# A selective-scan kernel: buffers named by the written schedule, y stored by pieces, late loads planned with a longer landing

## The chip, the cores and the metric

The kernel runs on one core of a Trainium2 chip. The time is the device time of one execution in microseconds; the number quoted for a kernel is the median of its runs. A core has five engines that each work through their own queue of instructions in order: PE (TensorE: matmuls and transposes, with its weight loads shown apart as PEld), DVE (VectorE), ACT (ScalarE), POOL (GpSimd) and SP (SyncE, which here only issues DMAs). Sixteen DMA engines move the data between memory and SBUF.

## The reference

The input x is 8 images of 64 x 64 positions with 96 channels. The first layer is a state-space block on a group-normalised x:

```
xz = x @ in_proj_w.T;  xin, z = split(xz)                 # 192 channels each
xc = silu(depthwise_conv3x3(xin))
xs = [xc by rows, xc by columns, and both reversed]       # K = 4 directions, 4096 positions
dts, Bs, Cs = split(x_proj_weight[k] @ xs[k])             # 6 + 16 + 16 rows
delta = softplus(dt_projs_weight[k] @ dts + bias)
h[t] = h[t-1] * exp(delta[t] * A) + (delta[t] * u[t]) * B[t]    # for each of 192 channels and N = 16 states
y[t] = sum over n of h[t, n] * C[t, n]  + D * u[t]
out = (layernorm(sum of the four y) * silu(z)) @ out_proj_w.T
x = x + out
```

A second layer follows: linear attention without softmax, and a two-layer feed-forward net whose products are rounded to an 8-bit float. By far the most work is the recurrence of h: 8 images x 4 directions x 192 channels x 16 states, each over 4096 positions.

## The kernel before

**Three passes.** Pass 1 (`pass1`, L274) normalises, projects and convolves, and writes u (the input of the scan), z and xd (the rows of dts, B and C) to memory; B and dt are also written split into three bf16 parts ("split", L244). Pass 2 (`pass2`, L548) does the scans and writes y for each image in two orders, o = 0 (by rows) and o = 1 (by columns). Pass 3 (`pass3`, L939) reads y and z and does all the rest.

**Tiling of pass 2.** A tile has 128 channels on the partitions and T = 1024 positions. Two images (a pair) have 2 x 192 = 384 channels, which makes three chunks: c = 0 and c = 1 hold 128 channels of one image each, and c = 2 holds the last 64 of both. So there are 4 pairs x 3 chunks = 12 chunks. A chunk has 4 directions k (order o = k % 2; k = 2, 3 reversed) of 4 pieces each, in all 192 pieces of 16 states n. "Piece 189" counts from 0.

**One piece.** `prepare` (L596) loads xb (B in three bf16 parts) and u, lets PE bring B to the other axis (ACT copies it to bT), lets POOL form du = delta * u, and PE and ACT transpose it to duT. `deltas_of` (L645) loads xdt, and makes delta by a matmul and a softplus on ACT. Then for each state n:

- `decay` (L720): ACT forms da = exp(delta * a), 128 x 1024.
- `products` (L759): PE fills a PSUM buffer "wide" with delta*u*B. There are three ways. ACT (`scaled`, L730) or POOL (`scaled_by_pool`, L746) forms x or xg from duT and bT, and PE transposes it, 8 transposes, after which the scan reads it; or PE spreads B over the channels with two matmuls and DVE multiplies by du in place.
- `scan` (L783): DVE runs the recurrence with one scan instruction per state into h, and so empties the "wide" buffer.
- for each two states: `carries` (L807, ACT copies the last column for the next piece), `times_c` (L822, POOL multiplies h by C in the tile c, which `load_c` (L708) loaded with C's rows repeated over all partitions, 1 MB), and `sum_over_n` (L836, PE adds the products up in the PSUM tile acc by transposing matmuls).

`take_acc` (L878): when a piece's sum is whole, ACT copies acc to its place in the SBUF tile y0 or y1 (`ys[o]`). Directions 0 and 1 leave it there. Directions 2 and 3 begin their sum with what is there and write back the total; after the fourth piece, `store_y` (L894) stores the whole of `ys[o]`, all 4096 positions. That is 2 MB to one image in c < 2, in runs of 512 B, and 1 MB to each of two images in c = 2, in runs of 256 B. All DMAs of this pass go through SP's queue (the very first loads through POOL's).

**Late work.** The x projection of image 7 and the splits of images 5 to 7 are done inside pass 2, beside the scans, by `late_x_projection` (L678) and `late_split` (L700). They share two single buffers, "late" (ux, bs) and "late2" (xd, bq).

**The order of work.** Nothing is scheduled at run time. `weave` (L148) plays the kernel through as a plan: each unit is a generator that yields the engine it wants next, the cost in us, the delay until its result is to be had (0.3 where none is given) and, where it takes a buffer, the pool's `Slots`. At each step the unit that can begin first goes next, and its instructions are recorded. `InOrder` (L85) then ties each engine to exactly this order. `Slots.when` (L138) tells the plan when the next buffer is free; it takes buffers in rotation, so the buffer of the allocation `count` earlier:

```python
        return 0.0 if self.taken < self.count else self.ends.get(self.taken + 1 - self.count)
```

The plan doesn't name the buffer, though: `take` (L571) asks the framework's pool of `bufs=count` for a tile, and the pool chooses by its own account. There are 4 da, 3 h, 4 x, 1 xg, 6 c, and in PSUM 3 wide and 1 acc (L556). Where the plan sees PE idle, `keep_busy` (L583) adds matmuls with a zero weight.

Of the kernel before, what the change touches and what calls it, by code (L numbers as in the profile page):

```python
# [39 lines left out]
PSUM = bass.MemoryType.PSUM  # L40
DRAM = bass.MemoryType.DRAM

P = 128
NB, HH, WW, C = 8, 64, 64, 96
# [7 lines left out]
NPC = L // T  # L52
NT = T // P
# [16 lines left out]
def chunk_rows(pair, c):  # L70

    b0 = 2 * pair
    if c < 2:
        return [(slice(0, P), b0 + c, slice(0, P))]
    return [(slice(64 * j, 64 * j + 64), b0 + j, slice(P, DI)) for j in range(2)]
# [9 lines left out]
class InOrder:  # L85


    def __init__(self, tc, engine):
        self.tc, self.engine, self.last = tc, engine, None
# [42 lines left out]
class Slots:  # L132
# [5 lines left out]
    def when(self):  # L138

        if self.held:  # L140
            return None
        return 0.0 if self.taken < self.count else self.ends.get(self.taken + 1 - self.count)

    def release(self, which, end):
        self.ends[which] = end


def weave(units, room, finished, between=None):  # L148

    free, clock = {}, 0.0
    waiting = {kind: [u for u in units if u[0] == kind] for kind in room}
    opened, ended, active = {kind: 0 for kind in room}, {kind: set() for kind in room}, []
    while True:  # L160
        for kind, todo in waiting.items():
            while opened[kind] < len(todo) and (opened[kind] < room[kind] or opened[kind] - room[kind] in ended[kind]):
                _, rank, unit = todo[opened[kind]]
                active.append([clock, rank, kind, opened[kind], unit, next(unit)])
                opened[kind] += 1
        best = None
        for at in active:
            while at[5][0] not in ENGINES and at[5] in finished:
                at[0] = max(at[0], finished[at[5]])
                at[5] = at[4].send(None)  # L170
            if at[5][0] not in ENGINES or (len(at[5]) > 3 and at[5][3].when() is None):
                continue
            begin = at[0] if len(at[5]) < 4 else max(at[0], at[5][3].when())
            key = (max(begin, free.get(at[5][0], 0.0)), at[1])
            if best is None or key < best[0]:
                best = key, at
        if best is None:
            assert not active and all(opened[kind] == len(todo) for kind, todo in waiting.items())
            return
        at = best[1]  # L180
        engine, cost, delay = (*at[5], 0.3)[:3]
        if len(at[5]) > 3:
            at[5][3].taken += 1
        clock = best[0][0]
        if between is not None:
            between(engine, clock - free.get(engine, 0.0))
        free[engine] = clock + cost
        at[0] = clock + cost + delay
        try:
            at[5] = at[4].send(at[0])  # L190
        except StopIteration:
            active.remove(at)
            ended[at[2]].add(at[3])
# [47 lines left out]
    return (a_neg, dsum, dt_b, dt_w, sel, sel2), load_dt_w  # L241


def split(engines, pool_of, cost, src, row, rows, pieces, at, dst):  # L244

    act, pool, sp = engines
    wide, used = GRP, rows * pieces
    yield "sp", 0.7, 4.0
    bq = pool_of.tile([P, wide], F32, name="bq", tag="late2")
    src = src[row : row + rows].rearrange("r (s t) -> (r s) t", s=pieces)  # L250
    sp.dma_start(bq[0:used], src[:, at : at + wide])
    yield "act", 0.6
    bs = pool_of.tile([P, NS, wide], BF16, name="bs", tag="late")
    act.copy(bs[0:used, 0, :], bq[0:used])
    yield "pool", cost
    pool.tensor_sub(bq[0:used], bq[0:used], bs[0:used, 0, :])
    yield "act", 0.6
    act.copy(bs[0:used, 1, :], bq[0:used])
    yield "pool", cost
    pool.tensor_sub(bs[0:used, 2, :], bq[0:used], bs[0:used, 1, :])  # L260
    yield "sp", 0.9
    half = used // 2
    for k2 in range(2):
        to = dst[k2].rearrange("e n (s t) -> (n s) e t", s=pieces)[:, :, at : at + wide]
        sp.dma_start(to, bs[half * k2 : half * (k2 + 1)])


def splits(b, o, b_d, dt_d):

    return [(0, 2 * N, 4, at, b_d[b][o]) for at in (0, GRP)] + [(DT0, 2 * R, 8, 0, dt_d[b][o])]  # L270
# [3 lines left out]
def pass1(ctx, tc, g, load_dt_w, ident, mhalf, engines, w_xp, u_d, z_d, xd_d, b_d, dt_d):  # L274
    nc = tc.nc
    pe, dve, act, pool = engines
    sp = InOrder(tc, nc.sync)
# [3 lines left out]
    two = ctx.enter_context(tc.tile_pool(name="p1two", bufs=2))  # L281
# [242 lines left out]
    def after(key, unit):  # L524
        yield key
        yield from unit

    units = []
    for pair in range(NB // 2):
        batches = (2 * pair, 2 * pair + 1)  # L530
        for b in batches:
            units += [("stats", statistics(b, q)) for q in range(NG)]
            units.append(("norm", group_norm(b)))
            units += [("proj", projection(b, q)) for q in range(NG)]
        for c in ORDER:
            units.append(("conv", convolution(pair, c)))
        for b in batches:
            for o in range(2 if b < LATE_X else 0):
                units += [("xproj", x_projection(b, o, q)) for q in range(NG)]
                if b < LATE:  # L540
                    units += [("split", after(("xd", b, o), split((act, pool, sp), two, 4.4, xd_d[b][o], *w))) for w in splits(b, o, b_d, dt_d)]
    units.append(("later", later_loads()))
    room = {"later": 1, "proj": 4, "norm": 1, "stats": 3, "xproj": 4, "split": 2, "conv": 3}
    weave([(kind, (list(room).index(kind), i), unit) for i, (kind, unit) in enumerate(units)], room, done)
# [3 lines left out]
def pass2(ctx, tc, g, ident, engines, fixed, w_xp, u_d, xd_d, b_d, dt_d, y_d):  # L548
# [3 lines left out]
    pe, dve, act, pool = engines  # L552
    sp = InOrder(tc, nc.sync)
    two = ctx.enter_context(tc.tile_pool(name="p2two", bufs=2))
    three = ctx.enter_context(tc.tile_pool(name="p2three", bufs=SOFT + 1))
    room = {"da": 4, "h": 3, "x": 4, "xg": 1, "c": 6, "wide": 3, "acc": 1}  # L556
    slots = {name: Slots(count) for name, count in room.items()}
    pools = {
        name: ctx.enter_context(tc.tile_pool(name=f"p2{name}", bufs=count, **({"space": PSUM} if name in ("wide", "acc") else {})))
        for name, count in room.items()  # L560
    }
    pieces = [
        (pair, c, k, NPC - 1 - i if k >= 2 else i) for pair in range(NB // 2) for c in range(3) for k in range(K) for i in range(NPC)
# [6 lines left out]

    def take(name, shape, dtype=F32):  # L571

        return pools[name].tile(shape, dtype, name=name), slots[name].taken

    def one_more(key, of, end):
        counts[key] = counts.get(key, 0) + 1
# [101 lines left out]
    def late_x_projection(b, o, q):  # L678

        yield "scans", 0  # L680
        pair, j = b // 2, b % 2
        cols = slice(q * GRP, (q + 1) * GRP)
        yield "sp", 1.8, 4.0
        ux = one.tile([P, 2, GRP], F32, name="ux", tag="late")
        sp.dma_start(ux[:, 0, :], u_d[b][o][0:P, cols])
        for i in range(2):
            sp.dma_start(ux[64 * i : 64 * i + 64, 1, :], u_d[2 * pair + i][o][P:DI, cols])
        yield "pe", 1.5, 0.2, slots["wide"]
        px, slot = take("wide", [P, T])
        for i, ty in enumerate((0, 1 + j)):  # L690
            pe.matmul(px[:, 0:GRP], w_xp[:, ty, o, :], ux[:, i, :], start=i == 0, stop=i == 1)
        end = yield "act", 0.58, 0.2
        xd = one.tile([P, GRP], F32, name="xd", tag="late2")[0 : 2 * NXD]
        act.copy(xd, px[0 : 2 * NXD, 0:GRP])
        slots["wide"].release(slot, end)
        end = yield "sp", 0.7, 3.0
        sp.dma_start(xd_d[b][o][:, cols], xd)
        one_more(("xd", b, o), NG, end)

    def late_split(b, o, which):  # L700

        yield "scans", 0
        if b >= LATE_X:
            yield "xd", b, o
        yield from split((act, pool, sp), one, 1.25, xd_d[b][o], *which)
        one_more(("split", b), 6, 0.0)

    def load_c(at, m):  # L708
# [169 lines left out]
    def take_acc(at):  # L878
        pair, c, k, pc = pieces[at]
        o = k % 2  # L880
        yield "sum", at
        end = yield "act", 0.95, 0.1
        if at % (K * NPC) == 0:
            for i in range(2):
                ys[i] = one.tile([P, NBLK, P], F32, name=f"y{i}")
        acc, slot = made["acc"]
        dst = ys[o][:, pc * NT : (pc + 1) * NT, :]
        act.copy(dst, acc)
        slots["acc"].release(slot, end)
        if k >= 2 and at % NPC == NPC - 1:  # L890
            yield "sp", 7.5, 6.0
            store_y(ys[o], o, chunk_rows(pair, c))

    def store_y(y, o, parts):  # L894
        for part, b, ch in parts:
            if o == 0:
                sp.dma_start(y_d[b][0].rearrange("(i p) d -> p i d", p=P)[:, :, ch], y[:, :, part])
            else:

                rows = y_d[b][1].rearrange("(h i w) d -> w h i d", w=2, h=HH)  # L900
                for w in range(2):
                    sp.dma_start(rows[w][:, :, ch], y[w * HH : (w + 1) * HH, :, part])

    units = []
    for at, (pair, c, k, pc) in enumerate(pieces):
# [334 lines left out]
```

## Time and profile before

| | us |
|---|---|
| median of 3 runs | 9894.99 (9894.46 to 9900.35) |
| profiled execution | 9906.51 |
| its span | 9904.5 |
| pass 1, until DVE's first scan | 683.5 |
| scans of pass 2 (683.5 to 9209.1) | 8525.6 |
| from the last scan to the end | 695.4 |

In the span DVE is busy for 94%, ACT for 92%, POOL for 91%, PE for 80%. The scans take 2.32 us each with a carried start value (2304 of them) and 2.26 us without (768); POOL's product with C takes 4.55 us (1536). The granted PE clock is 0.963 in the mean.

A line of a wait list reads: engine and what it writes, "<-" what ended the wait, total us, number of waits, the longest. A line of a timeline reads: start, duration, engine, source line (L93, the recording helper, for nearly all), operation, out<-in, shapes, count, and in brackets the idle time before it with what ended it. A line of a table of windows gives the window, its length, and for PE, PEld, DVE, ACT and POOL the busy time and the number of instructions, then the granted clock, the busy share of the DMA engines and GB/s. Lines for SP are DMA issues.

### The profile page before, as it was taken

The page shows a single profiled execution, that of the slowest core. Times are in us where ns is not written, and L with a number is a line of the kernel's source. Part 1 is how long each engine was busy: PE and PEld are TensorE (multiplying, and loading weights), DVE is VectorE, ACT ScalarE, POOL GpSimd, SP SyncE. Part 2 cuts the span into 40 slices and gives each one's busy share as a digit, 9 for nine tenths or more (in the row PEclk, how much of TensorE's full clock was granted, in tenths as well). Part 3 has the DMA queues.
Part 4 walks back from the last instruction along what each step waited for, and adds up shares of the span by engine and source line. Part 5 has one row for each costly group of instructions (what it writes and reads, how often), then busy time and mean ns, then how long its engine had stood idle before and what let it go on. Part 6 is the DMA issues. An engine that isn't in the chain of part 4 may idle for free.

```text
span 9904.5 us, 162493 instructions
## 1 busy us (share of the span) xinstructions
PE 7951.6 (80%) x57093; PEld 6231.6 (63%) x57093; DVE 9325.3 (94%) x6971; ACT 9119.9 (92%) x21486; POOL 9004.1 (91%) x2911
## 2 busy tenths in 40 slices
PE   7768888888887887888888888878878878878787
PEld 3336666666666666666666666666666666666676
DVE  7879999999999999999999999999999999999687
ACT  5769999999999999999999999999999999999797
POOL 1449999999999999999999999999999999999677
PEclk8889999999999999999999999999999999999898
DMA  5776776789986776799976766899867667999663
GB/s 165 236 224 214 227 238 219 232 216 212 217 225 214 227 228 218 225 219 208 212 227 213 229 222 218 226 209 207 222 218 225 222 213 227 215 209 206 189 185 107
DMA packets 937134, 2120.70 MB, mean 214 GB/s; under 512 B 275371, under 2 KB 423628, under 8 KB 934786
## 3 DMA queue, kind: packets, MB, share of 16 engines
q1 hardware_dynamic: 933514, 2108.96, 76.1%
q8 instruction: 456, 7.47, 0.3%
q14 instruction: 356, 2.92, 0.1%
q0 software_dynamic: 432, 0.94, 0.0%
q10 hardware_dynamic: 2376, 0.40, 0.0%
HBM read 1934.36 MB, written 175.66 MB: 213 GB/s over the span
## 4 chain that ended last, share of the span: by engine, by line
ACT 28%; DVE 25%; issue 19%; PE 11%; POOL 8%; DMA 7%; SPq 1%; DVEq 0%; POOLq 0%; ACTq 0%
DVE h L93 18%; ACT x L93 12%; ACT da L93 10%; POOL c L93 6%; DVE wide L93 5%; PE wide L93 4%; PE acc L93 3%; DMA c<-xd_d 3%; PE pa L93 1%; ACT L93 1%; PE px L93 1%; PE mm L93 1%; DVE u L93 1%; DMA xb<-b_d 1%; ACT y L93 1%
## 5 line engine op out<-in xcount | busy, mean ns | idle before, releaser
L93 POOL TENSOR_TENSOR c<-c,h 128x2048 f32<-128x2048 f32 x1536 | 6962.1, 4554 | 177.7 <-DVE h L93 129.8
L93 DVE TENSOR_TENSOR_SCAN h<-da,carry,wide 128x1024 f32<-128x1024 f32 x2304 | 5255.7, 2330 | 147.7 <-PE wide L93 103.9
L93 ACT ACTIVATE x<-duT,bT 128x128 f32<-128x128 f32 (+1 forms) x14336 | 4198.0, 368 | 13.6 <-PE wide L93 12.3
L93 ACT ACTIVATE da<-delta,a_neg 128x1024 f32<-128x1024 f32 x3072 | 3501.1, 1144 | 139.8 <-DVE h L93 135.6
L93 PE MATMUL acc<-ident,c 128*128 128x128 f32 x24576 | 3165.9, 279 | 380.9 <-POOL c L93 366.7
L93 PEld LDWEIGHTS acc<-ident,c 128*128 128x128 f32 x24576 | 2811.3, 143 | 777.3 <-POOL c L93 649.2
L93 PE MATMUL wide<-ident,x 128*128 128x128 f32 x11264 | 1523.3, 280 | 483.5 <-DVE h L93 449.9
L93 DVE TENSOR_TENSOR_SCAN h<-da,wide 128x1024 f32<-128x1024 f32 x768 | 1703.1, 2268 | 59.0 <-PE wide L93 37.1
L93 PEld LDWEIGHTS wide<-ident,x 128*128 128x128 f32 x11264 | 1268.1, 143 | 768.0 <-DVE h L93 331.9
L93 DVE TENSOR_TENSOR wide<-du,wide 128x1024 f32<-128x1024 f32 x1216 | 1462.4, 1209 | 91.3 <-PE wide L93 66.8
L93 PE MATMUL acc<-sel,zero 96*128 96x512 bf16 x3941 | 1066.0, 380 | 0.0
L93 PE MATMUL wide<-xb,sel 96*128 96x512 bf16 x2432 | 733.2, 386 | 291.8 <-DVE h L93 277.1
L93 POOL TENSOR_TENSOR xg<-duT,bT 128x512 f32<-128x512 f32 (+1 forms) x640 | 892.7, 1409 | 24.1 <-PE wide L93 12.1
L93 PE MATMUL wide<-ident,xg 128*128 128x128 f32 x3584 | 495.4, 284 | 162.4 <-DVE h L93 155.8
L93 PEld LDWEIGHTS <-zero 96*128 96x128 bf16 x3941 | 383.2, 98 | 304.8 <-issue 5.5
L93 PEld LDWEIGHTS wide<-ident,xg 128*128 128x128 f32 x3584 | 416.3, 146 | 249.5 <-issue 149.2
L93 PEld LDWEIGHTS <-sel 96*128 96x128 bf16 x2432 | 220.8, 99 | 458.0 <-issue 226.7
L93 POOL TENSOR_TENSOR du<-delta,u 128x1024 f32<-128x1024 f32 x192 | 457.2, 2381 | 41.2 <-DMA u<-u_d 20.9
L93 DVE SCALAR_TENSOR_TENSOR u<-xpad,conv_w,u 128x4096 f32<-128x4096 f32 x96 | 451.2, 4700 | 1.9
L93 ACT COPY carry<-h 128x2 f32<-128x2 f32 x1152 | 214.4, 186 | 139.9 <-DVE h L93 134.2
L93 POOL TENSOR_TENSOR bq<-bq,bs 128x512 f32<-128x512 f32 (+1 forms) x48 | 120.2, 2506 | 172.1 <-ACT bs L93 163.5
L93 ACT ACT_TABLE_LOAD x196 | 251.5, 1283 | 22.9 <-DMA b2q_raw<-in_b 19.4
(150 smaller groups left out, 6239.5 us busy)
## 6 DMA issues: line engine op xcount, KB each, us to landing
c<-xd_d SPq DMA_DIRECT2D x1024, 1024.0 KB
c<-xd_d SPq DMA_DIRECT2D x1024, 512.0 KB
u<-u_d SPq DMA_DIRECT2D x127, 512.0 KB
xdt<-dt_d SPq DMA_DIRECT2D x1146, 36.0 KB
xb<-b_d SPq DMA_DIRECT2D x382, 96.0 KB
u<-u_d SPq DMA_DIRECT2D x128, 256.0 KB
zs<-z_d SPq DMA_DIRECT2D x128, 256.0 KB
y_d<-y SPq DMA_DIRECT2D x24, 1024.0 KB
```

The lines of the kernel that those rows point to most:

```text
L93: ins = getattr(self.engine, op)(*args, **kwargs).ins
```

## The change

It touches the pass of the scans alone, in three ways.

*Buffers.* `Slots` is replaced there by `Buffers`, which keeps the planned time at which each buffer comes free, hands out the one that is free first, and knows its number. Each buffer is then a tile with a tag of its own, so the built kernel uses just the buffer that the plan meant.

*Stores.* After each piece of directions 2 and 3, `take_acc` stores that quarter of y, in place of the whole after the fourth piece. The plan gives each store 3.0 us of SP (7.5 before) and lets it begin 2.0 us after ACT's copy (0.1 before).

*Landing times.* The plan counts 12 us (4 before) from the issue of ux and of a late bq to its use, and 25 us (3 before) for the landing of a late xd. The early splits of pass 1 keep their 4.0.

```diff
+    def take(self):
+        self.taken += 1
+
     def release(self, which, end):
         self.ends[which] = end
+
+class Buffers:
+
+    def __init__(self, count):
+        self.free, self.taken, self.held = [0.0] * count, None, False
+
+    def when(self):
+        return None if self.held else min((end for end in self.free if end is not None), default=None)
+
+    def take(self):
+        self.taken = self.free.index(self.when())
+        self.free[self.taken] = None
+
+    def release(self, which, end):
+        self.free[which] = end
...
         if len(at[5]) > 3:
-            at[5][3].taken += 1
+            at[5][3].take()
...
-def split(engines, pool_of, cost, src, row, rows, pieces, at, dst):
+def split(engines, pool_of, cost, landing, src, row, rows, pieces, at, dst):
...
-    yield "sp", 0.7, 4.0
+    yield "sp", 0.7, landing
...
-    slots = {name: Slots(count) for name, count in room.items()}
+    slots = {name: Buffers(count) for name, count in room.items()}
     pools = {
-        name: ctx.enter_context(tc.tile_pool(name=f"p2{name}", bufs=count, **({"space": PSUM} if name in ("wide", "acc") else {})))
-        for name, count in room.items()
+        name: ctx.enter_context(tc.tile_pool(name=f"p2{name}", bufs=1, **({"space": PSUM} if name in ("wide", "acc") else {})))
+        for name in room
     }
...
-        return pools[name].tile(shape, dtype, name=name), slots[name].taken
+        which = slots[name].taken
+        return pools[name].tile(shape, dtype, name=name, tag=f"{name}{which}"), which
...
-        yield "sp", 1.8, 4.0
+        yield "sp", 1.8, 12.0
         ux = one.tile([P, 2, GRP], F32, name="ux", tag="late")
...
-        end = yield "sp", 0.7, 3.0
+        end = yield "sp", 0.7, 25.0
         sp.dma_start(xd_d[b][o][:, cols], xd)
...
-        yield from split((act, pool, sp), one, 1.25, xd_d[b][o], *which)
+        yield from split((act, pool, sp), one, 1.25, 12.0, xd_d[b][o], *which)
...
-        end = yield "act", 0.95, 0.1
+        end = yield "act", 0.95, 2.0
...
-        dst = ys[o][:, pc * NT : (pc + 1) * NT, :]
-        act.copy(dst, acc)
-        slots["acc"].release(slot, end)
-        if k >= 2 and at % NPC == NPC - 1:
-            yield "sp", 7.5, 6.0
-            store_y(ys[o], o, chunk_rows(pair, c))
+        of = slice(pc * NT, (pc + 1) * NT)
+        act.copy(ys[o][:, of, :], acc)
+        slots["acc"].release(slot, end - 2.0)
+        if k >= 2:
+            yield "sp", 3.0, 6.0
+            store_y(ys[o], o, of, chunk_rows(pair, c))
...
-                sp.dma_start(y_d[b][0].rearrange("(i p) d -> p i d", p=P)[:, :, ch], y[:, :, part])
+                sp.dma_start(y_d[b][0].rearrange("(i p) d -> p i d", p=P)[:, of, ch], y[:, of, part])
...
-                    sp.dma_start(rows[w][:, :, ch], y[w * HH : (w + 1) * HH, :, part])
+                    sp.dma_start(rows[w][:, of, ch], y[w * HH : (w + 1) * HH, of, part])
```

More of the change, by code (lines that the diff above doesn't have):

```diff
@@ L540, in pass1 @@
                 if b < LATE:
-                    units += [("split", after(("xd", b, o), split((act, pool, sp), two, 4.4, xd_d[b][o], *w))) for w in splits(b, o, b_d, dt_d)]
+                    units += [("split", after(("xd", b, o), split((act, pool, sp), two, 4.4, 4.0, xd_d[b][o], *w))) for w in splits(b, o, b_d, dt_d)]
     units.append(("later", later_loads()))
@@ L886, in take_acc, with store_y @@
         acc, slot = made["acc"]
-        dst = ys[o][:, pc * NT : (pc + 1) * NT, :]
-        act.copy(dst, acc)
-        slots["acc"].release(slot, end)
-        if k >= 2 and at % NPC == NPC - 1:
-            yield "sp", 7.5, 6.0
-            store_y(ys[o], o, chunk_rows(pair, c))
-    def store_y(y, o, parts):
+        of = slice(pc * NT, (pc + 1) * NT)
[4 more added lines that the diff above has]
+            store_y(ys[o], o, of, chunk_rows(pair, c))
+    def store_y(y, o, of, parts):
         for part, b, ch in parts:
             if o == 0:
-                sp.dma_start(y_d[b][0].rearrange("(i p) d -> p i d", p=P)[:, :, ch], y[:, :, part])
+                sp.dma_start(y_d[b][0].rearrange("(i p) d -> p i d", p=P)[:, of, ch], y[:, of, part])
             else:
```

## The prediction

> **What bounds the kernel now.** I read the page first, then a table of busy time with one row for each of the twelve chunks of the scan pass (683.5 to 9209.1 us; from first to last scan), then the waits of DVE, PE and SP inside that pass, then the timeline at the longest gaps. Page, part 1:
>
> ```profile
> PE 7951.6 (80%) x57093; PEld 6231.6 (63%) x57093; DVE 9325.3 (94%) x6971; ACT 9119.9 (92%) x21486; POOL 9004.1 (91%) x2911
> ```
>
> No engine stands out over the whole span, so the chunk decides. The table's columns are window, length, busy us (instructions) of PE, PEld, DVE, ACT, POOL, granted clock, DMA share, GB/s. First pair 0's third chunk (c=2), then chunks c=0 and c=2 of pair 2:
>
> ```profile
> 2090.70:2840.10 749.40, 601.57 (x4328) 468.62 (x4329) 702.15 (x369) 719.59 (x1963) 719.92 (x246) 0.97 0.96 213
> ...
> 4970.30:5663.30 693.00, 567.66 (x4298) 457.06 (x4298) 680.85 (x354) 657.88 (x1462) 675.41 (x177) 0.99 0.70 223
> ...
> 6357.60:7089.10 731.50, 589.99 (x4283) 471.36 (x4283) 700.26 (x369) 716.50 (x1959) 712.26 (x240) 0.96 0.94 211
> ```
>
> See that in a c<2 chunk DVE is the fullest (680.9 of 693.0) with POOL 5 us behind it, while in a c=2 chunk ACT and POOL are fuller than DVE and the DMA engines are at 0.94 to 0.96. A chunk can't get shorter than its fullest engine. Length less fullest engine, summed over the twelve rows: 128 us in the eight c<2 chunks, 77 us in the four of c=2. That is all that an order of work can win in this pass. DVE's idle time in it is 275 us. Who ends it:
>
> ```profile
> DVE h L93 <- PE wide L93: 140.9, 105, 9.7
> DVE wide L93 <- PE wide L93: 66.8, 64, 4.2
> DVE h L93 <- ACT da L93: 22.0, 22, 3.7
> ...
> PE wide L93 <- DVE h L93: 1019.0, 1384, 3.1
> PE wide L93 <- DMA xb<-b_d: 48.5, 15, 7.1
> ...
> SPq L93 <- PE acc L93: 5686.0, 1342, 12.5
> ```
>
> 208 us of DVE's idle time waits for PE to fill a PSUM buffer "wide" (three of them), and PE waited for DVE to empty one. The longest gap, in piece 189 (of 0 to 191), starts on the SP queue (two lines of SP's timeline, then PE and DVE):
>
> ```profile
> 9032.16 8.23 SPq L93 DMA_DIRECT2D y_d<-y  x2
> 9070.55 3.94 SPq L93 DMA_DIRECT2D xb<-b_d  x2
> ...
> 9089.29 0.38 PE L93 MATMUL wide<-sel,xb 96*128 96x32 bf16 x8 [7.06 <-DMA xb<-b_d]
> 9091.59 2.35 DVE L93 TENSOR_TENSOR_SCAN h<-da,carry,wide 128x1024 f32<-128x1024 f32 x1 [9.69 <-PE wide L93]
> ```
>
> A whole y of 2 MB is stored at once, the DMA share stays at 0.93 to 1.05 from 9030 to 9090, and xb takes 18.7 us to land.
>
> **What the skill says.** (1) The Trainium skill, "Perfetto Trace Analysis", Identifying the Most-Contended Engine: the same gap repeating on the engine that should be full can mean that memory for the next tile is short. The trace agrees: 169 of DVE's waits are for "wide". (2) "DMA: Bandwidth & Descriptors", Queues, rings and completion order: an engine takes descriptors in the order of their ring. The 18.7 us of xb behind the store agree. (3) The same page, Specifications: under 512 B a transfer falls short of line rate. The trace's DMA packets: 8192 of 256 B for a c=2 store of 2 MB took 149 us, that is 9.3 us of all 16 engines; 4096 of 512 B in c<2 took 111 us, or 6.9. (4) "Perfetto Trace Analysis", DMA Optimizations: splitting lets parts start sooner if the engines are generally idle. They are at 0.70 in c<2, but not in c=2, so this alone promises nothing there.
>
> **The change part by part.** *Buffers.* I compared the order and the addresses of the built programs. x, xg, h, c and acc come round at the same distance in both (x 4, h 3, c 6), so naming them costs and saves nothing; da barely moves (4 in 2860 against 2902 of 3072). "wide" does: 2980 of its 3664 tiles took the third-last one's buffer, now 2304, because the planner hands out the one free first. For each product DVE reads, I noted what emptied its buffer last and how much DVE work stands between, and gave each class the mean gap that the timeline of before has ahead of it (gaps over 4 us apart):
>
> - buffer emptied by the DVE instruction just before, so PE's work lies open. Matmul products 42 x 0.751 us = 31.5; now 7, 5.3. Transposed products 34 x 1.378 = 46.9; now 14, 19.3. Saved 53.8.
> - transposed, with one or two instructions (about 2 us) between: 374 at 0.085 us, now 197: 14.6 saved.
> - emptied by ACT (bT, delta, duT, xd): matmul products 254 at 0.103 (two long gaps left out), now 132: 12.5 saved. Transposed 284 at 0.108, now 360: 8.2 lost.
> - all others: 4 saved.
>
> Sum 77 us. With means taken for c<2 and c=2 apart: 48 in c<2, 25 in c=2. Pieces of 0.6 to 1.3 us, on the path in c<2 because DVE is fullest there.
>
> *Stores.* 24 stores of a y become 96 of a quarter; 48 DMA instructions become 192. Bytes and packet sizes stay. Issue on SP: a c=2, o=0 store took 8.2 to 9.0 us for two DMAs, so a quarter about 2.1: the same sum. At worst 144 more at the shortest seen, 0.4 to 0.55 us: 72 us on a queue that waits 5686 us for c buffers, so nothing. Each store waits for ACT's copy of y; behind it stand c loads, then xdt, xb and u. SP waited for ACT y 44.4 us in 19 waits, 2.3 each; 96 would be 225 us, again under the 5686. POOL's waits hold no late c load. Without that cover xb suffers first: in the built order it is issued two sums over n (about 11 us) ahead of its use in 117 of 191 pieces before, 127 after. Gain: the long gaps behind a whole store, 5.2, 6.6 and 9.7 (fourteenth piece of c=2 in pairs 1 to 3), 7.3 (pair 0, second piece) and 4.2 (after the c=2, o=1 store): 33 us, 29 of them in c=2. DMA work per piece in the second half of a c=2 chunk rises by 9.3/4 = 2.3 us of 45, spread rather than heaped.
>
> *Longer landing.* It moves ACT and PE work behind late loads (ux, bq) further back; before, ACT waited 8.7 us once for bq, with a DVE gap of 6.3 in pair 0. But the built order has bq directly behind the xd store, in the same buffer, 6 times instead of 3, and SP waits about 4.5 us each time (49.4/11). Between 13 gained and 13 lost; I take nothing, and so do not count that 6.3.
>
> *Handover to the last pass.* ACT's last y copy ends at 9222.7, SP stores y for 7.2 us, then loads for pass 3; POOL waits 19.2 us for yo. A quarter stores in about 2: 5 us gained, DMA backlog aside.
>
> *Sum.* c<2: 48 + 4 = 52 of the 128 available. c=2: 25 + 29 = 54, but the headroom is 77 and ACT and POOL would have to run at 99%; I take three quarters, 40. 52 + 40 + 5 = 97. The profiled execution took 9906.5 us (span 9904.5 and 2 around it): 9809.5. The median lies 11.5 below the profiled one, so 9798; I say **9800**.
>
> **Rivals.** *The waits pass on to POOL and ACT.* POOL is busy 675 to 688 in a c<2 chunk against DVE's 681, and ACT 716 in c=2. If half of c<2 (26) and a quarter of c=2 (10) survive, with the handover: 41 gained, 9854. Against it: each steady c<2 chunk still has 5 us left under DVE.
> *The naming changes nothing.* The pool's own choice was the rotation for 2980 of 3664 tiles, and gaps may come from late PE work instead. Then only the stores count: three quarters of 29, 4 and 5: 31, so 9864. Against it: every one of the 76 buffers emptied just before showed a gap over 0.3 us.
> *Slower: buffers behind ACT.* 492 products now follow a buffer that ACT empties (538 before), and 173 transposed ones follow a bT (70 before), whose filling hangs on the xb load. ACT is 95% busy in the pass; if its copies come late, PE's transposes (about 1 us) lie open. Their mean wait was 0.156 us and I count on 0.107. At 0.40 they cost 144 us more and the kernel takes 9945. The run is slower by over 0.2% from a mean of 0.34 on. Against it: ACT waits rather than being waited for (DVE waits for ACT da 22 us in all).
> *No change,* within 0.2% (20 us, about what a measurement here can tell): gains and losses cancel.
>
> **How the numbers follow.** Likeliest case 0.57, its own range 9765 to 9835 (all of the claims and the 13 of the landing, or two thirds of them); POOL and ACT 0.14; naming nothing 0.08; no change 0.09; slower 0.12. So faster 0.79, same 0.09, slower 0.12. The range 9765 to 9892 takes in all but the slower case and a thin tail below.
>
> **What would show it.** DVE's idle time in the pass falls from 275 to about 185 us, its waits for PE wide from 208 to about 115. c<2 chunks take about 687 to 698 us, c=2 chunks of pairs 1 to 3 about 719. No DVE gap over 4 us is left in the fourteenth pieces of c=2; xb's share of PE's waits falls below 20 us. The longest gaps left are in pair 0's c=2, around bq. POOL's wait for yo at the handover falls to about 14. Wrong would be: chunks no shorter though waits for "wide" fell (POOL or ACT took over), or many new waits of DVE for PE behind a bT.

## The result and the profile after

The changed kernel takes 9742.2 us (median of 4 runs, 9720.0 to 9745.1) against 9897.7 before (4 runs): 155 us less, a ratio of 0.9837, interval 0.982 to 0.9854. I had said 9800, with a range from 9765 to 9892: the sign was right, and the time lies below the range.

The profiled execution of after is the fastest of the four, 22 us below the next, at a granted clock of 0.976 (the others: 0.970 or 0.971), and the profiled one of before (9906.5) lies 9 us above its median. Between these two the span falls by 186 us, and some of that is not the change. By stretches, in us:

| | before | after |
|---|---|---|
| pass 1, until the first scan | 683.5 | 676.9 |
| eight c<2 chunks | 5588.7 | 5488.4 |
| four c=2 chunks | 2936.8 | 2874.6 |
| after the last scan | 695.4 | 678.2 |

So about 100 us come from c<2, where I had counted on 52, 62 from c=2 (40), and 17 from what follows the scans (5). These are single executions: two kernels below whose time is that of before within 8 us (longer landing alone; all buffers but "wide" named) have 5580 and 5584 in c<2 and 2945 and 2933 in c=2, so some 10 us of such a sum mean nothing. Pass 1 is the same code in both; in the kernels below, too, it ends anywhere between 677 and 689. Page of after, part 1:

```profile
PE 7892.6 (81%) x57076; PEld 6117.4 (63%) x57076; DVE 9304.7 (96%) x6971; ACT 9099.7 (94%) x21486; POOL 8998.3 (93%) x2911
```

As before, the chunks decide. The table of windows of after, for the three chunks shown of before (pair 0's c=2, then c=0 and c=2 of pair 2), and then the whole pass, of before and of after:

```profile
2052.93:2779.26 726.33, 588.86 (x4289) 452.86 (x4289) 699.65 (x370) 717.80 (x1963) 716.50 (x246) 0.99 0.97 218
...
4872.85:5556.65 683.80, 564.35 (x4297) 450.61 (x4297) 678.77 (x353) 657.88 (x1468) 675.88 (x177) 1.00 0.71 226
...
6241.17:6957.79 716.62, 582.51 (x4286) 454.16 (x4286) 699.58 (x369) 712.35 (x1956) 711.50 (x240) 0.99 0.97 216
```

```profile
683.50:9209.10 8525.60, 6917.69 (x51544) 5530.41 (x51543) 8250.80 (x4287) 8140.41 (x19564) 8285.62 (x2402) 0.98 0.79 219
```

```profile
676.90:9039.90 8363.00, 6872.08 (x51527) 5428.35 (x51526) 8228.84 (x4287) 8121.39 (x19565) 8277.90 (x2402) 0.99 0.81 224
```

See that the steady c<2 chunk is now 5 us longer than DVE's work (12 before), and the c=2 chunk 4 us longer than ACT's (15 before): of the 128 us of headroom in c<2, 100 are gone, and 62 of the 77 in c=2. DVE runs the same 4287 instructions in the pass, yet its busy time fell from 8250.8 to 8228.8; I come back to these 22 us. Waits of DVE, PE and SP inside the pass, after:

```profile
DVE h L93 <- PE wide L93: 44.2, 45, 2.2
DVE h L93 <- ACT da L93: 40.7, 43, 3.5
DVE wide L93 <- PE wide L93: 15.7, 22, 1.8
```

```profile
PE wide L93 <- DVE h L93: 817.6, 1220, 2.7
...
PE wide L93 <- ACT bT L93: 25.1, 31, 2.2
PE wide L93 <- DMA xb<-b_d: 23.2, 15, 5.3
```

```profile
SPq L93 <- PE acc L93: 5599.0, 1360, 9.5
...
SPq L93 <- ACT y L93: 30.4, 47, 1.6
```

DVE's waits for PE to fill "wide" fell from 208 us in 169 waits to 60 in 67. Its idle time in the pass is 134 us in 243 gaps, where it was 275 in 453; the idle time that ACT's da ends rose from 22 to 41 us and is now as large as the first group. PE's wait for xb has halved (48.5 before). SP still waits 5599 us for PE, so its more numerous store instructions cost nothing there.

The same place as before, the fourteenth piece of the last c=2 chunk (scans from 8909.2 us on): the quarter of y stored before it, the loads of C and the xb that PE needs next on SP's timeline, then PE and DVE, of after:

```profile
8873.55 1.49 SPq L93 DMA_DIRECT2D y_d<-y  x2
...
8886.22 24.63 SPq L93 DMA_DIRECT2D c<-xd_d  x12
8910.89 1.05 SPq L93 DMA_DIRECT2D xb<-b_d  x2
```

```profile
8924.38 0.35 PE L93 MATMUL wide<-sel,xb 96*128 96x32 bf16 x8 [1.42 <-DMA xb<-b_d]
```

```profile
8920.39 6.81 DVE L93 TENSOR_TENSOR_SCAN h<-da,carry,wide 128x1024 f32<-128x1024 f32 x3
8927.11 1.20 DVE L93 TENSOR_TENSOR wide<-du,wide 128x1024 f32<-128x1024 f32 x1
```

A quarter is issued in 1.5 us, where the whole took 8.2. The xb has 13.5 us from its issue to PE's use (18.7 before), PE waits 1.4 us for it (7.1 before), and DVE works on: in this piece it has no gap over 0.15 us. Loads of C stand between the store and this xb, as before (fourteen DMAs then, twelve now), so the store is not all that it waits behind. The gap of 9.7 us is gone; the longest gap in the whole pass is 3.5 us.

At the handover to the last pass, POOL's first sum, before and after:

```profile
9238.41 1.80 POOL L93 TENSOR_TENSOR y<-y,yo 128x768 f32<-128x768 f32 x1 [19.21 <-DMA yo<-y_d]
```

```profile
9058.01 1.80 POOL L93 TENSOR_TENSOR y<-y,yo 128x768 f32<-128x768 f32 x1 [11.29 <-DMA yo<-y_d]
```

It starts 18.1 us after the last scan; before, 29.3.

### The profile page after: what moved, and what is told of

It reads as the page before. It is cut to its first block, busy times and chain, and to the rows that moved or that the text cites. A ratio compares the mean times of both kernels' runs of the same rounds, so it can differ in the third digit from the quotient of the medians.

```text
span 9718.1 us, 162759 instructions
## 1 busy us (share of the span) xinstructions
PE 7892.6 (81%) x57076; PEld 6117.4 (63%) x57076; DVE 9304.7 (96%) x6971; ACT 9099.7 (94%) x21486; POOL 8998.3 (93%) x2911
## 5 line engine op out<-in xcount | busy, mean ns | idle before, releaser
L93 PEld LDWEIGHTS acc<-ident,c 128*128 128x128 f32 x24576 | 2758.2, 141 | 900.1 <-POOL c L93 764.4
L93 PE MATMUL wide<-ident,x 128*128 128x128 f32 x11264 | 1497.6, 277 | 383.1 <-DVE h L93 309.1
L93 PEld LDWEIGHTS wide<-ident,x 128*128 128x128 f32 x11264 | 1248.5, 141 | 653.1 <-DVE h L93 194.0
L93 PEld LDWEIGHTS wide<-ident,xg 128*128 128x128 f32 x3584 | 394.6, 142 | 312.8 <-issue 249.8
L93 PE MATMUL wide<-ident,du 128*128 128x128 f32 x1536 | 205.7, 277 | 83.0 <-DVE h L93 63.5
```

Source lines behind the costliest of these rows:

```text
L93: ins = getattr(self.engine, op)(*args, **kwargs).ins
```

## The experiments

Each kernel was timed against the kernel before on the same chip; differences are taken within such a group of runs, whose medians of before were 9890.7 (the first four kernels), 9892.6 (the next four), 9886.6 (three) and 9894.9 (the last).

### Each part alone

**First-free buffers, each named; stores and landings as before.**

```diff
-    slots = {name: Slots(count) for name, count in room.items()}
+    slots = {name: Buffers(count) for name, count in room.items()}
...
-        return pools[name].tile(shape, dtype, name=name), slots[name].taken
+        which = slots[name].taken
+        return pools[name].tile(shape, dtype, name=name, tag=f"{name}{which}"), which
```

> Before with the named, first-free buffers alone; y stored whole, landings as before. Theory 1 (waits of PE's products for a wide buffer are most of the gain): the counts of products by what emptied their buffer last are nearly those of the whole change (9, 22, 197, 148, 341 against 7, 14, 205, 132, 360), so 80 to 115 us below before, DVE's waits for PE wide near 100 us, while the long gaps behind a whole y store (5 to 10 us, fourteenth piece of c=2) stay. Theory 2 (the bursts of the stores are most of it): under 45 us below before.

Measured: 9810.5, ratio 0.9921 (0.9906 to 0.9936), 80 us less. The c<2 chunks sum to 5508 (before 5589), those of c=2 to 2925 (2937): nearly all the gain is in c<2. In c=2 long gaps remain, but not where expected: none over 3.2 us is left in a fourteenth piece, and there are three of 7.8 to 9.1 us in the second piece of a c=2 chunk. The one in piece 81, in SP's timeline, then PE's, then DVE's, of this kernel:

```profile
4179.52 8.30 SPq L93 DMA_DIRECT2D y_d<-y  x2
...
4198.10 22.94 SPq L93 DMA_DIRECT2D c<-xd_d  x14
4222.85 2.69 SPq L93 DMA_DIRECT2D xb<-b_d  x2
```

```profile
4240.37 0.38 PE L93 MATMUL wide<-sel,xb 96*128 96x32 bf16 x8 [7.46 <-DMA xb<-b_d]
```

```profile
4243.82 1.23 DVE L93 TENSOR_TENSOR wide<-du,wide 128x1024 f32<-128x1024 f32 x1 [8.93 <-ACT x L93]
```

A whole y, then fourteen C loads, then xb: from 4200 to 4240 the DMA share is 1.03 to 1.04 by the table of windows, and xb takes 15 us from the end of its issue to PE's use.

**Quarter stores alone.**

```diff
-        if k >= 2 and at % NPC == NPC - 1:
-            yield "sp", 7.5, 6.0
-            store_y(ys[o], o, chunk_rows(pair, c))
+        if k >= 2:
+            yield "sp", 3.0, 6.0
+            store_y(ys[o], o, of, chunk_rows(pair, c))
```

(with the delay of 2.0 us after ACT's copy that belongs to it)

> Before with y of the reversed directions stored by quarters alone; buffers by the pools in rotation. Theory 1: 35 to 65 us below before (33 us of long gaps, 11 at the handover, some 15 from the order that the plan makes around the stores: products whose buffer was emptied just before fall from 42 and 34 to 27 and 28); no DVE gap over 4 us in the fourteenth pieces of c=2. Theory 2: over 100 us below before.

Measured: 9860.8, ratio 0.997 (0.9958 to 0.9981), 30 us less, just under the 35 to 65 expected: c<2 unchanged (5588), c=2 27 less (2910), the tail 680 instead of 695. Of the gaps of the fourteenth pieces none over 1.1 us is left.

**Longer landing alone.**

```diff
-        yield "sp", 1.8, 4.0
+        yield "sp", 1.8, 12.0
...
-        end = yield "sp", 0.7, 3.0
+        end = yield "sp", 0.7, 25.0
```

(and 12.0 for 4.0 in the late splits)

> Before with the longer landing times of late loads alone. Theory 1: no more than 13 us either way, since the order still puts bq right behind the store of xd. If the landing times matter beside the rest: over 20 us below before, with pair 0 and pair 1 shorter and pairs 2 and 3 unchanged.

Measured: 9897.9, ratio 1.001 (1.0001 to 1.0019). Nothing, or a few us lost.

The three differences, −80, −30 and +7, sum to −103; the whole change is −155. Some 50 us belong to no part alone.

### What it is in the naming

**All buffers named in rotation.** Here the plan is untouched, and every engine's instructions stand in the same order as before. Only the buffer is the one that the plan meant: number (taken − 1) mod count.

```diff
+        which = slots[name].taken
-        return pools[name].tile(shape, dtype, name=name), slots[name].taken
+        return pools[name].tile(shape, dtype, name=name, tag=f"{name}{(which - 1) % room[name]}"), which
```

> Before with every buffer named, but handed out in the rotation that the plan of before counts on, so the built kernel uses just the buffers of that plan. If the pools' departure from the plan was the harm (332 plus 342 of 3664 wide tiles), this gains as much as first-free named buffers, 80 to 115 us. If the choice of the buffer that is free first is the gain, this gains only what the counts say: products laid open 42 to 11 and 34 to 32, others alike, 20 to 35 us.

Measured: 9817.9, ratio 0.9927 (0.9912 to 0.9942), 73 us less, with c<2 at 5512.5 and c=2 at 2933.7. The framework's pool had departed from the rotation for 681 of the 3664 tiles of "wide", and this cost almost as much as first-free buffers gain. My classes don't foresee the size: by their counts over the whole pass (buffers emptied by the DVE instruction just before: 42 to 11 of the multiplies, 34 to 32 of the transposed ones), this order should gain 23 us. In c<2 these two go from 31 to 0 and from 25 to 10, and DVE's gaps ahead of them from 54.8 to 15.6 us. Most of the rest of c<2's 76 us lies ahead of products behind ACT, whose number hardly changes (363 to 359) and whose gaps still fall from 35 to 10 us. In c=2 the transposed ones rise from 9 to 22, and the chunks there, which DVE doesn't fill, don't lengthen.

**Only "wide" named, and all but "wide" named**, both in rotation, with the order of before (for the second kernel `named` holds the six others):

```diff
+    named = ("wide",)
+        tag = f"{name}{(which - 1) % room[name]}" if name in named else name
+        return pools[name].tile(shape, dtype, name=name, tag=tag), which
```

> As e4_rotation, but of the pools only the PSUM buffers wide are named (in rotation); da and all others stay with their pools. Every engine's order of instructions is that of before. If wide carries the gain of naming: as e4_rotation, 60 to 85 us below before. If da (where 208 of 3072 tiles left the rotation) carries it: within 20 us of before.

> The complement: all pools but wide are named in rotation, the order is that of before. If wide carries the gain: within 20 us of before. If da carries it: 60 to 85 us below.

Measured: 9817.3, ratio 0.9925 (0.991 to 0.994), for "wide" alone; 9892.4, ratio 1.0 (0.9991 to 1.0008), for all the others. DVE's waits inside the pass, first with only "wide" named:

```profile
DVE h L93 <- PE wide L93: 113.5, 87, 8.1
DVE h L93 <- ACT da L93: 21.4, 23, 2.4
DVE wide L93 <- PE wide L93: 19.8, 23, 4.2
```

and with all but "wide" named:

```profile
DVE h L93 <- PE wide L93: 134.1, 97, 7.3
DVE wide L93 <- PE wide L93: 62.4, 58, 4.2
DVE h L93 <- ACT da L93: 24.7, 22, 5.0
```

With "wide" named, DVE's waits before its multiplies fall from 62 to 20 us, those before its scans by 20. So the naming acts through the three PSUM buffers alone, and it does so without any change of order or of choice in the plan. In the built programs the three lie at the same PSUM addresses as before, so their place is not the cause; nor is the tag itself, since the others gained nothing by theirs. Nor is the granted clock: at 0.966 in the mean, runs of before took 9892 and 9899 us, and runs with only "wide" named 9817 and 9822.

### Why the whole is more than its parts

**The whole change without the longer landings.**

> The whole change without the longer landing times. If they are worth nothing (alone they cost 7 us): 9735 to 9755 us, as the whole change. If they only pay once the other waits are gone: over 20 us slower than the whole change, in pairs 0 and 1.

Measured: 9742.7, ratio 0.985 (0.9834 to 0.9867), 150 us less: the landing times are worth nothing here either. Its profiled execution (9742.3) is a better stand-in for the median of the whole change than that one's own: first scan at 684.2, c<2 5488.2, c=2 2886.1, tail 682.1. Against the profiled execution of before that is 100 in c<2, 51 in c=2 and 13 in the tail, 14 us more than the medians differ by.

**The whole change, but planned and named in rotation** (`Slots` and its number in place of `Buffers`):

```diff
-    slots = {name: Buffers(count) for name, count in room.items()}
+    slots = {name: Slots(count) for name, count in room.items()}
...
+        return pools[name].tile(shape, dtype, name=name, tag=f"{name}{(which - 1) % room[name]}"), which
```

> The whole change, but the named buffers are handed out in rotation, not the one free first. If naming alone is the gain of the buffers, this is within 20 us of the whole change. If the gain beyond the parts (buffers 80, stores 30, landing -7, together 155) comes from first-free buffers letting the plan fit the stores in: 9775 to 9800 us.

Measured: 9810.2, ratio 0.992 (0.9905 to 0.9935), 82 us less: neither of the two cases foreseen. Rotation and quarter stores together can't be told from rotation alone. Against before on the same chip:

| us | pool's choice | named, rotation | named, first free |
|---|---|---|---|
| whole stores | 0 | −73 | −80 |
| quarter stores | −30 | −82 | −155 (−150 without landings) |

With whole stores the choice of the first free one adds 7 us, less than can be told (each of these differences is good to about 15 us), with quarter stores 68 to 73. With rotation the quarter stores do give c=2 their 38 us (2934 to 2895), but c<2 loses 33 (5512 to 5545): the ACT copies and stores now stand at other places in the plan, and products whose buffer DVE emptied just before rise in c<2 from 10 to 35; the gaps ahead of these from 15.6 to 43.3 us. With first-free buffers (the whole change) they are 16, with 19.0 us.

**First free for "wide" alone**, all else in rotation:

```diff
-    slots = {name: Buffers(count) for name, count in room.items()}
+    slots = {name: Buffers(count) if name == "wide" else Slots(count) for name, count in room.items()}
```

> The whole change, but only the PSUM tiles "wide" are handed out by first free; da, h, x, xg, c and acc are planned and named in rotation. With all in rotation and the same stores the time was 9810, with all by first free 9743. If it is the choice of the wide buffer that gives those 67 us, this kernel takes 9742 to 9762: in the built order 34 products still lie open behind the DVE instruction just before (21 with all by first free, 57 with all in rotation), some 0.8 us each, so 10 us more than the whole change, and the c<2 chunks sum to some 5495. Rival: the freedom of the other buffers (da above all, whose rotation holds ACT's exponentials back) lets the plan take the stores in. Then the time stays at 9800 to 9812 and the c<2 chunks at some 5540.

Measured: 9751.9, ratio 0.9863 (0.9846 to 0.9879), 135 us less, and c<2 5486.3, the same as with everything first free. So the choice of the "wide" buffer is what takes up the quarter stores in c<2. The 15 to 20 us missing against the whole change are at the edge of what can be told; they lie in c=2 (2900), and what the freedom of the other buffers does there was not taken apart.

DVE's waits inside the pass, in rotation and then with first free for "wide", both with quarter stores:

```profile
DVE h L93 <- PE wide L93: 96.7, 68, 8.8
DVE h L93 <- ACT da L93: 28.2, 25, 3.1
DVE wide L93 <- PE wide L93: 20.5, 31, 1.8
```

```profile
DVE h L93 <- ACT da L93: 40.7, 38, 3.4
DVE h L93 <- PE wide L93: 39.2, 41, 2.3
DVE wide L93 <- PE wide L93: 38.7, 41, 5.8
```

### What bounds the chunks of c=2 now

ACT and POOL are at 99% of the c=2 chunks after the change. Two kernels give part of their work to DVE, which has 17 us of room: in two, then in four pieces of sixteen, one state that ACT scales and one that POOL scales go to DVE's multiply.

```diff
+def ways(at, c):
+    by_act, by_pool = WAYS[c // 2]
+    if c == 2 and at % 16 in (4, 10):
+        return by_act[1:], by_pool[:-1]
+    return by_act, by_pool
```

(`ways(at, c)` in place of `WAYS[c // 2]` in both places; (2, 6, 9, 13) for four pieces)

> The whole change, and in c=2 chunks two pieces of sixteen (the fifth and the eleventh) give one state each from ACT and one from POOL to DVE: 2 x 2 x (1.208 - 0.085) = 4.5 us more for DVE in a chunk, 2 x 4.04 = 8.1 less for ACT, 2 x 2.04 = 4.1 less for POOL. If POOL and ACT bound these chunks (712 and 713 busy of 717, DVE 699), each falls by about 4, the four by 12 to 18, and the kernel takes about 9727. Rival: what is left in c=2 is the DMA engines' or the waits' and no engine's; then 9742 within 10. A third: DVE's waits for wide grow with the multiplies; then 9755 and more.

> The same in four pieces of sixteen: DVE 9.0 us more in a c=2 chunk (709), ACT 16.2 less (697), POOL 8.2 less (704). If the fullest engine bounds, DVE is it now and the chunks take some 713: gain 12 to 16, not twice that of two pieces, kernel 9728. Rivals as for two pieces: 9742 within 10 if the DMA engines bound; 9760 and more if DVE's waits for wide grow with its multiplies.

Measured: 9733.1, ratio 0.9842 (0.9828 to 0.9857), and 9726.6, ratio 0.9836 (0.9822 to 0.9851); the whole change has 0.9837. Neither can be told from it. The c=2 chunks of pairs 1 to 3 sum to 2144 and 2149, the whole change's to 2148. With four pieces ACT is busy for 9 to 11 us less in each of them (16 were expected) and POOL for 7 to 10 less, and the chunks kept their length. So taking work off the two fullest engines did not shorten them. That these were never the limit is not shown, since the same edit gives DVE 7 to 8 us more: with 705 to 707 it is now the fullest, 7 to 12 us under the length.

**DMA work taken out of c=2**, on top of the kernel with four pieces:

```diff
+        if len(parts) == 2:
+            return
+        b = parts[0][1]
-        for part, b, ch in parts:
+        for part, b, ch in parts + [(slice(0, 64), b, slice(P, DI))]:
```

> The kernel with four pieces of sixteen given partly to DVE, and with the c=2 stores of y left out: a c<2 store writes the 64 channels of its image's last part too (from its own first 64, so that part of y is not the reference's). That takes 18.6 us of all 16 DMA engines (2 stores of y of 9.3) out of each c=2 chunk, whose DMA share was 0.95 to 0.97, and brings it to some 0.94; c<2, at 0.71, takes 4 x 9.3 / 2 more per chunk. If the DMA engines are what keeps the c=2 chunks at 713 to 718 although no engine is fuller than 707, these fall to some 711 (DVE's 707 and what a steady c<2 chunk has left above DVE, 5), pair 0's below 725, and the kernel takes 9700 to 9712. If it is not the DMA engines but waits between engines, the chunks stay at 713 to 718 and the kernel within 10 of 9727.

Measured: 9714.7, ratio 0.982 (0.9804 to 0.9837); against the kernel with four pieces, each against its own before, 20 us less, where the two intervals overlap. The table of windows for pair 0's c=2 and pair 2's c=2, of the kernel with four pieces:

```profile
2058.33:2793.61 735.28, 593.76 (x4246) 463.96 (x4246) 707.35 (x377) 709.01 (x1905) 711.06 (x238) 0.96 0.97 217
6246.25:6964.62 718.37, 585.01 (x4223) 458.53 (x4223) 706.85 (x377) 702.91 (x1897) 702.52 (x232) 0.97 0.96 215
```

and of this one:

```profile
2057.51:2775.43 717.92, 586.75 (x4246) 459.16 (x4246) 706.97 (x377) 706.90 (x1905) 710.41 (x238) 0.98 0.98 218
6231.15:6948.01 716.86, 583.50 (x4223) 456.60 (x4223) 706.74 (x377) 702.86 (x1897) 701.87 (x232) 0.97 0.94 210
```

Pair 0's chunk, the one with late work beside it, is 17 us shorter, within 8 of its fullest engine. That fits DMA work as the limit there, but it is one execution of each, and it is not shown: this chunk took 726 us in the profiled execution of the whole change, with all its DMA work, at a granted clock of 0.99 in place of 0.96, and 738 in that of the kernel without the longer landings. In pairs 1 to 3 the sum stays (2147), at DMA shares of 0.93 to 0.95 in place of 0.95 to 0.97: there taking off DMA work changed nothing, as taking off work of ACT and POOL had not. What keeps these chunks some 10 us above the fullest engine, in gaps of which none is over 3 us in the last kernel, stays open. No kernel that computes the whole beats the changed one by more than can be told.

## Why the prediction was right and wrong

**Buffers: the right place, the wrong reason.** That "wide" is the buffer concerned and the others cost and save nothing was right (all but "wide" named: ratio 1.0). But I put the gain down to the planner's choice of the first free one. With rotation, where all but the first three of the 3664 tiles take the third-last one's buffer, more than before (2980), 73 of the 80 us are there. My count of 2304 against 2980 thus measured the wrong thing: with whole stores both first free and rotation gain when the built kernel follows the plan, and what had cost was the pool's departure from it. The sentence of the Trainium skill that I had drawn on ("Perfetto Trace Analysis"; it stands in its section Optimization Strategy) takes a repeated gap as a sign that memory for the next tile may be short. Here the memory stayed at three buffers, and 75 us hung on which of them was taken. The rival "the naming changes nothing" falls with the same runs. The other rival, that transposed products behind ACT lie open, is refuted in its size: the 492 products behind ACT have 59.4 us of gaps, 0.121 each where I had counted on 0.107 and the break-even was 0.34 (the 360 transposed ones 0.111, for 0.108).

**c<2: 52 said, 100 measured.** The term mis-sized is the class sum of 48. DVE's gaps in c<2 by class, from the first scan on, before and after:

| c<2, us | before | after |
|---|---|---|
| emptied by DVE just before | 54.8 | 19.0 |
| emptied by ACT | 36 | 24 |
| one or two instructions between, transposed | 17.9 | 6.6 |
| all other products | 13.9 | 0.5 |
| scans after their own multiply, and the like | 17.7 | 6.0 |

The first three rows gain 59, not far from the 48 entered. The last two gain 25, of which I had entered 4 at most: I took the gaps whose class the change doesn't touch as fixed, and they went too. That a late product makes the next ones late, so that gaps with ample work between were the echo of those without, fits this, but is argued and not shown. The rest is a term that I left out: in the records consecutive DVE instructions overlap by 85 ns (2542 such pairs in c<2 before, mean 85 ns), and across a gap they do not, so each gap costs its idle time and some 85 ns more. Three neighbours of after, each beginning before the one ahead of it has ended:

```profile
8870.10 1.21 DVE L93 TENSOR_TENSOR wide<-du,wide 128x1024 f32<-128x1024 f32 x1
8871.22 2.28 DVE L93 TENSOR_TENSOR_SCAN h<-da,wide 128x1024 f32<-128x1024 f32 x1
8873.41 1.21 DVE L93 TENSOR_TENSOR wide<-du,wide 128x1024 f32<-128x1024 f32 x1
```

DVE's busy time in the pass fell by 22 us with the same instructions: 15 by more overlap (326 to 341 us, with 210 fewer gaps) and 7 because the single instructions were recorded a little shorter, for which the runs show no cause. In c<2 it fell by 16, 12 of them by overlap. Idle 83 and busy 16 are the 100.

**c=2: 54 cut to 40; 62 measured, 51 in the kernel that stands for the median.** The cut failed. I took a quarter off because ACT and POOL would have to run at 99%; they do (712 of 717), and the chunks fell all the same. The stores' part was nearly right: 29 said, 27 for quarter stores alone. I had read the Trainium skill ("Perfetto Trace Analysis", DMA Optimizations: splitting helps if the engines are generally idle) as promising nothing at a DMA share of 0.95; the runs show that quarters gained there all the same, 27 us alone: what comes behind a quarter on the queue is held up for less, as with the xb shown above (18.7 and 13.5 us).

**The parts don't add up.** I added buffers and stores as if apart. Each alone gives 80 and 30, without the landings both give 150: some 40 us that I had put at nothing (uncertain by some 25, by the three intervals). First-free buffers alone met the long gaps behind whole stores in c=2 (12 gained there), and quarter stores need a free choice of "wide" to be taken in without exposing products in c<2. That the buffers alone came near the 73 of my sum is luck: some 80 in c<2 for 48, some 12 in c=2 for 25.

**Handover: 5 said; POOL's first sum comes 11 us earlier after the last scan**, since the wait for yo fell from 19.2 to 11.3 (I had said 14) and the copies and stores ahead of it are shorter; the tail is 678 to 684 with quarter stores and 689 to 695 with whole ones, in all kernels. **Landing: nothing, as said.** **SP: nothing, as said;** not the same issue time, though: the stores take SP 143 us in all where they took 102, inside the bound of 72 more, and under the cover named.

**The signs I had named.** No gap over 4 us in the fourteenth pieces, c=2 chunks of pairs 1 to 3 about 719 (713 to 719): right. The longest gap is in pair 0's c=2, but after ACT's da and not around bq. xb's share of PE's waits is 23, not below 20. DVE idle 134 and not 185, waits for "wide" 60 and not 115, c<2 chunks 684 to 689, at and under the low end of 687 to 698: all three wrong on the side of the gain that was missing from the sum.

**The step that failed** is thus the sum. By place, it fell short mainly in c<2, by 48 of the 58 between 97 and 155: each class was given its mean gap of before, and the other gaps went too. By part, it fell short in adding: alone, buffers and stores gave 110, about what I had for them before the cut (73 for buffers; 33 and 5 for stores and handover), and the rest came only from both together. The range was too narrow below because its lower end allowed for "all of the claims" and the landing, but not for claims that were themselves too small.

## What to carry to other kernels

Where an order of work is planned ahead, make the built kernel use the buffers that the plan meant: an allocator that picks another of three equal PSUM buffers now and then cost this kernel 75 us with no instruction moved. When gaps on the fullest engine are priced by class, don't take the classes that the change leaves alone as fixed, and count for each gap the overlap between neighbours that it breaks. Test two edits together as well as apart before adding their gains: here choice and stores gave 150 together, 110 apart.

## What the runs showed of the hardware that I had not expected

Neighbouring DVE instructions overlap by 85 ns in the records, so the same 4287 instructions are busy for less when they stand closer: 15 of the 22 us by which DVE's busy time fell. Engines at 99% of a chunk's length did not keep it from falling from 731.5 to 716.6 us, and giving them room afterwards (9 to 11 us on ACT, 7 to 10 on POOL, with 7 to 8 more on DVE) left the c=2 chunks of pairs 1 to 3 at 2149 us in the sum. At a DMA share of 0.93 to 0.95 in place of 0.95 to 0.97 these three kept their length, too. Whether the DMA work limits pair 0's c=2 chunk, at 0.97, stays open.
